# One in 42 runs of sixteen history positions fetched by SyncE, row by row, in the user stage of a recommender kernel

## The chip, the cores and the metric

The kernel runs on one core of one Trainium2 chip. The metric is the device time of one execution in microseconds; the median of three runs of the kernel before is 30,856.08 us (30,855.88 to 30,856.29). One further execution was taken with the hardware profiler, and every duration in this document that has a row of a profile beside it is from such an execution.

The engines are called as the profile calls them: PE is the TensorE, DVE the VectorE, ACT the ScalarE, POOL the GpSimd, SP the SyncE. SP does no arithmetic; in this kernel it issues plain DMAs.

## The reference, cut to what matters

There are 50,001 items and 16,384 users with 100 history positions each.

```python
# per item: two neighbour attentions over 32 neighbours
a_sus = _neighbor_attn(E_in, near_full)          # 50001 x 32
a_inf = _neighbor_attn(E_out, near_full)
# per user and history position
h = concat([E_hist[history], a_sus[history], a_inf[history]])   # 16384 x 100 x 128
t = concat([E_tgt[target],  a_inf[target],  a_sus[target]])     # 16384 x 128
z = relu(einsum('bld,hd->blh', h * t[:, None, :], W1) + b1)
exp_A = exp(einsum('blh,h->bl', z, W2[0])) * mask
attn = exp_A / (sum(exp_A, -1) ** 0.5)[:, None]
s = sum(h * attn[..., None])                     # one number
pred = dot(s, t) / (norms);  return sigmoid(pred)
```

`mask` leaves out positions whose item is the target or item 0.

## The kernel before, in words

There are two stages, one after the other.

**The item stage** works out, for all items, a row of 128 floats (64 of `E_hist`, 32 and 32 of the two attentions) and writes it to `table` in DRAM, and a second such row to `ttab` for targets. POOL gathers 30 of the 32 neighbours by indirect DMAs (L215); the other two are copied column by column from a transposed copy of the embeddings in SBUF by ACT and DVE (L229), whose addresses come from registers. The registers are loaded 32 at a time from SBUF (L189). A branch in which SP would fetch neighbours is in the code but its share is set to nought. The change leaves this stage as it is.

**The user stage** is where the change lies. The 16,384 users are laid out as 128 partitions by 128 columns; the code calls one column, which is 128 users, c, and this document calls it "user c" where the order of the work is meant. The 100 history positions of a column are cut into groups of `LW = 8`: twelve full groups and one of four, thirteen in all. The loop goes over all groups (c, g) in order, in a software pipeline of three steps:

- `gather(c, g)`: for each of the group's positions, POOL issues an indirect DMA that fetches 128 rows of 512 bytes from `table`, one for each partition (L438), into a buffer `h` of which there are six.
- `turn(c, g)`: PE transposes each position (L453), DVE multiplies by the transposed target (L455, `xT`) and sums the rows of `h` (L458, `hsum`).
- `hidden` one group later: PE multiplies by W1 (L473), ACT applies the relu (L474). `scored` two groups later: PE multiplies by W2 (L482); after the last group of a column, ACT and DVE take the exponential, the mask and two sums (L488 to L492).

Target rows of a column are one more POOL gather (L400), issued half a column ahead. The history itself, which holds the indices of the gathers, is loaded by SP for four columns at a time (L396, `hidx`, two buffers), when the target rows of a block's first column are asked for.

A column is thus 101 POOL gathers. Each engine works through its own instructions in order; a scheduling layer inserts the waits. Buffers are freed for POOL when PE and DVE have read them. The DMAs that SP issues share eight semaphores in rotation.

Of the kernel before, what the change touches and what calls it, by code (L numbers as in the profile page):

```python
# [10 lines left out]
F32 = mybir.dt.float32  # L11
I32 = mybir.dt.int32
U8 = mybir.dt.uint8
E = mybir.EngineType
AF = mybir.ActivationFunctionType
ALU = mybir.AluOpType
AX = mybir.AxisListType

P = 128
ITEMS = 50001  # L20
# [3 lines left out]
D = 128  # L24
HID = 128
B = 16384
L = 100
# [20 lines left out]
UC = B // P  # L48
BSUB = 4
LG = 4  # L50
NG = L // LG


@with_exitstack
def kernel(
# [13 lines left out]
    nc = tc.nc  # L69
# [12 lines left out]
    table = dram.tile([ROWS, D], F32, name="table")  # L82
# [30 lines left out]
    with (  # L113
# [84 lines left out]
        def gather(s):  # L198
            it, j = divmod(s, NSUB)
            nidx = its[it][0]  # L200
            v = n_v.tile([P, K, 2, G], F32, name="v")
            g = [n_g.tile([P, P], F32, name=f"g{a}") for a in range(NAUX)]
            subs[s] = {"v": v, "g": g}
            k1 = K - NAUX - 1
            by_sp = s * SPNUM % SPDEN < SPNUM
            if by_sp:
                for i0 in range(0, P, NREG):
                    vals = registers(s, 0, E.SP, i0, 0, (ITEMS - 1) * 8 * G)
                    for i in range(NREG):
                        nc.sync.dma_start(  # L210
                            v[i0 + i : i0 + i + 1, k1].rearrange("p t d -> p (t d)").bitcast(U8),
                            egeo_b[:, ds(vals[i], 8 * G)],
                        )
            for k in range(k1 if by_sp else k1 + 1):
                nc.gpsimd.indirect_dma_start(  # L215
                    out=v[:, k].rearrange("p t d -> p (t d)"),
                    out_offset=None,
                    in_=egeo,
                    in_offset=bass.IndirectOffsetOnAxis(ap=nidx[:, j, k : k + 1], axis=0),
                )  # L220
# [145 lines left out]
    hist_v = history.rearrange("(p i j) l -> i p j l", p=P, j=BSUB)  # L366
# [2 lines left out]
    tidf = const.tile([P, UC], F32, name="tidf")  # L369
    nc.vector.tensor_copy(tidf, tidx)  # L370
    with (
        tc.tile_pool(name="u_in", bufs=2) as u_in,
        tc.tile_pool(name="u_t", bufs=2) as u_t,
        tc.tile_pool(name="u_h", bufs=6) as u_h,
        tc.tile_pool(name="u_x", bufs=2) as u_x,
        tc.tile_pool(name="u_s", bufs=2) as u_s,
        tc.tile_pool(name="ps_t", bufs=2, space=bass.MemoryType.PSUM) as ps_t,
        tc.tile_pool(name="ps_z", bufs=2, space=bass.MemoryType.PSUM) as ps_z,
        tc.tile_pool(name="ps_s", bufs=2, space=bass.MemoryType.PSUM) as ps_s,
    ):  # L380
        users = {}
        hists = {}
        LW = 2 * LG
        NW = -(-L // LW)
        in_order = mybir.DependencyInfo(
            mybir.DependencyClass.NoSync, mybir.DependencyReason.DATA
        )

        def width(g):
            return min(LW, L - g * LW)  # L390

        def target_rows(c):

            if c % BSUB == 0:
                hidx = u_in.tile([P, BSUB, L], I32, name="hidx")
                nc.sync.dma_start(hidx, hist_v[c // BSUB])  # L396
                hists[c // BSUB] = hidx

            t = u_t.tile([P, D], F32, name="t")
            nc.gpsimd.indirect_dma_start(  # L400
                out=t,
                out_offset=None,
                in_=ttab[0:ITEMS, :],
                in_offset=bass.IndirectOffsetOnAxis(ap=tidx[:, c : c + 1], axis=0),
            )
            users[c] = {"t": t, "hidx": hists[c // BSUB][:, c % BSUB, :]}

        def target_work(c):
            u = users[c]
            t = u["t"]  # L410
            tT_ps = ps_t.tile([P, LG, P], F32, name="hT_ps")
            nc.tensor.transpose(tT_ps[:, 0, :], t, ident)
            tT = u_t.tile([D, 1, P], F32, name="tT")
            nc.vector.tensor_copy(tT[:, 0, :], tT_ps[:, 0, :])
            u["tT"] = tT
            nc.vector.tensor_reduce(tsum[:, c : c + 1], t, AX.X, ALU.add)
            junk = u_t.tile([P, D], F32, name="junk")
            nc.scalar.activation(junk, t, AF.Square, accum_out=tsq[:, c : c + 1])
            idf = u_s.tile([P, L], F32, name="idf")
            nc.scalar.copy(idf, u["hidx"])  # L420
            keep = u_s.tile([P, L], F32, name="keep")
            nc.vector.tensor_scalar(keep, idf, 0.0, None, ALU.not_equal)
            nc.vector.scalar_tensor_tensor(
                keep, idf, tidf[:, c : c + 1], keep, ALU.not_equal, ALU.mult
            )
            u["keep"] = keep
            u["hsum"] = u_s.tile([P, L], F32, name="hsum")
            u["score"] = ps_s.tile([P, L], F32, name="score")
            u["xT"], u["z"] = {}, {}

        def gather(c, g):
            u = users[c]
            h = u_h.tile([P, LW, D], F32, name="h")
            u["got", g] = []
            for q in range(width(g)):
                l = g * LW + q
                u["got", g].append(
                    nc.gpsimd.indirect_dma_start(  # L438
                        out=h[:, q, :],
                        out_offset=None,  # L440
                        in_=table,
                        in_offset=bass.IndirectOffsetOnAxis(ap=u["hidx"][:, l : l + 1], axis=0),
                    )
                )
            u["h", g] = h

        def turn(c, g):
            u = users[c]
            w = width(g)
            h = u.pop(("h", g))  # L450
            hT_ps = ps_t.tile([P, LW, P], F32, name="hT_ps")
            for q in range(w):
                nc.tensor.transpose(hT_ps[:, q, :], h[:, q, :], ident)  # L453
            xT = u_x.tile([D, LW, P], F32, name="xT")
            x = nc.vector.tensor_tensor(  # L455
                xT[:, 0:w, :], hT_ps[:, 0:w, :], u["tT"].to_broadcast([D, w, P]), ALU.mult
            )
            s = nc.vector.tensor_reduce(  # L458
                u["hsum"][:, g * LW : g * LW + w], h[:, 0:w, :], AX.X, ALU.add
            )  # L460

            tc.add_manual_dep(s.ins, x.ins.name, in_order, reason="after x")
            for q in u.pop(("got", g)):
                tc.declare_no_dep(s.ins, q.ins, reason="after x")
            u["xT"][g] = xT

        def hidden(c, g):
            u = users[c]
            xT = u["xT"].pop(g)
            z = u_x.tile([HID, LW, P], F32, name="z")  # L470
            for q in range(0, width(g), LG):
                z_ps = ps_z.tile([HID, LG, P], F32, name="z_ps")
                nc.tensor.matmul(z_ps, w1T, xT[:, q : q + LG, :], start=True, stop=True)  # L473
                nc.scalar.activation(z[:, q : q + LG, :], z_ps, AF.Relu, bias=b1_sb)  # L474
            u["z"][g] = z

        def scored(c, g):
            u = users[c]
            z = u["z"].pop(g)
            for q in range(width(g)):  # L480
                l = g * LW + q
                nc.tensor.matmul(  # L482
                    u["score"][:, l : l + 1], z[:, q, :], w2_sb, start=True, stop=True
                )
            if g < NW - 1:
                return
            ea = u_s.tile([P, L], F32, name="ea")
            nc.scalar.activation(ea, u["score"], AF.Exp)  # L488
            nc.vector.tensor_tensor(ea, ea, u["keep"], ALU.mult)  # L489
            nc.vector.tensor_reduce(den[:, c : c + 1], ea, AX.X, ALU.add)  # L490
            nc.vector.tensor_tensor(ea, ea, u["hsum"], ALU.mult)
            nc.vector.tensor_reduce(num[:, c : c + 1], ea, AX.X, ALU.add)  # L492
            del users[c]

        groups = [(c, g) for c in range(UC) for g in range(NW)]
        target_rows(0)
        for s in range(len(groups) + 2):
            if s < len(groups):
                c, g = groups[s]
                if g == 0:  # L500
                    target_work(c)
                if g == NW // 2 and c + 1 < UC:
                    target_rows(c + 1)
                gather(c, g)
                turn(c, g)
            if 1 <= s <= len(groups):
                hidden(*groups[s - 1])
            if s >= 2:
                scored(*groups[s - 2])
# [88 lines left out]
```

## Time and profile before

| | |
|---|---|
| median of the runs | 30,856.08 us |
| the profiled execution | 30,865.45 us |
| its span, first to last instruction | 30,863.6 us |
| user stage: first history gather starts | 14,704.9 us |
| user stage: last history gather starts | 30,845.2 us |
| POOL busy | 23,284.3 us, 75% of the span |
| PE busy (matmuls) | 13,340.6 us, 43% |
| DVE busy | 12,128.8 us, 39% |
| ACT busy | 7,843.2 us, 25% |
| TensorE clock granted in the user stage | 0.62 of full speed |

A row of a group of instructions reads: line, engine, operation, output and inputs by the program's names, count; then the busy time in us and the mean duration of one in ns; then the engine's idle time just before them and what ended most of it. "issue" is time in which the engine waited for nothing that the profile shows. A row of a line's view gives the minimum, median and maximum duration in ns, and the first and last start in us. SPq, ACTq and DVEq are the sequencers of these engines; what they do themselves (issuing a DMA, loading a register) is not counted as busy. In a timeline a row is start, duration (us), engine, line, operation, count, and in brackets the idle time before it. A row of a window has its bounds and length, and then the busy time and count of PE, of PE's weight load, of DVE, ACT and POOL, the granted clock, the busy share of the DMA engines and GB/s.

### The profile page before, as it was taken

Reading aid. Unit: us, or ns where it says so; the run is one execution under the profiler, and the core shown is the slowest. Engines: PE = TensorE matmul, PEld = TensorE weight load, DVE = VectorE, ACT = ScalarE, POOL = GpSimd, SP = SyncE. Lnnn points to the kernel's source line nnn. Section 1 sums busy time; section 2 is a strip of 40 time slices with the busy share of each in tenths; the row PEclk is TensorE's granted clock in tenths of the full one; section 3 lists DMA queues with packets and bytes.
Section 4 is the critical chain, followed back from the end, with each engine's and each line's share of the span. In section 5 each row is a group of like instructions: output and inputs, shape, how many; then the busy total and the mean of one; then the engine's idle time right before and its main releaser. Section 6 shows DMA issues by size and latency. Waiting matters only on the chain.

```text
span 30863.6 us, 246685 instructions
## 1 busy us (share of the span) xinstructions
PE 13340.6 (43%) x45932; PEld 7630.5 (25%) x45932; DVE 12128.8 (39%) x58485; ACT 7843.2 (25%) x56963; POOL 23284.3 (75%) x24664
## 2 busy tenths in 40 slices
PE   0000000000000000000778778877877877887787
PEld 0000000000000000000444444444444544454444
DVE  5555555555555555555222222222222222222222
ACT  4333333333333333333111111111111111111111
POOL 7777777777777777777777777777777777777777
PEclk9999999999999999999665666666566566656656
DMA  2111111111111111111222222222222222222221
GB/s 67 31 31 31 32 34 31 31 31 32 34 31 31 31 35 31 31 31 29 54 53 54 54 53 54 53 53 53 54 53 54 53 54 53 53 53 54 53 54 52
DMA packets 966199, 1351.82 MB, mean 44 GB/s; under 512 B 548416, under 2 KB 561280, under 8 KB 961696
## 3 DMA queue, kind: packets, MB, share of 16 engines
q0 software_dynamic: 789056, 1233.20, 17.1%
q10 hardware_dynamic: 103920, 51.31, 0.6%
q1 hardware_dynamic: 71664, 51.54, 0.6%
q14 instruction: 1192, 9.76, 0.1%
q8 instruction: 367, 6.01, 0.1%
HBM read 1295.95 MB, written 51.30 MB: 44 GB/s over the span
## 4 chain that ended last, share of the span: by engine, by line
POOL 56%; issue 23%; DMA 12%; PE 7%; DVE 1%; another core or an unknown queue 0%; ACT 0%; POOLq 0%; SPq 0%; ACTq 0%; DVEq 0%
POOL v L215 33%; POOL h L438 23%; DMA h<-table,hidx 10%; PE z_ps L473 3%; DMA v<-in_egeo_dram,nidx 2%; PE score L482 2%; PE hT_ps L453 2%; DVE xT L455 1%; DVE hsum L458 0%; DMA st<-in_egeo_dram 0%; PE pt L180 0%; POOL t L400 0%; POOLq L438 0%; ACT g L229 0%
## 5 line engine op out<-in xcount | busy, mean ns | idle before, releaser
L438 POOL DMA_INDIRECT h<-table,hidx x12800 | 12084.6, 944 | 3899.7 <-issue 3451.0
L215 POOL DMA_INDIRECT v<-in_egeo_dram,nidx x11730 | 11078.2, 944 | 3599.4 <-issue 3484.2
L453 PE MATMUL hT_ps<-ident,h 128*128 128x128 f32 x12800 | 5070.5, 414 | 3207.2 <-DMA h<-table,hidx 3025.5
L455 DVE TENSOR_TENSOR xT<-hT_ps,tT 128x1024 f32<-128x1024 f32 (+1 forms) x1664 | 1968.4, 1183 | 10942.7 <-PE hT_ps L453 10942.5
L234 PE MATMUL pt<-ident,g 128*128 128x128 f32 x782 | 363.9, 471 | 13297.0 <-DVE g L229 8118.8
L473 PE MATMUL z_ps<-xT,w1T 128*128 128x512 f32 x6400 | 5799.9, 1007 | 26.6 <-DVE xT L455 26.3
L229 ACT COPY g<-geoT 128x4 uint8 x50048 | 4919.0, 189 | 2153.7 <-issue 2152.4
L474 ACT ACTIVATE z<-z_ps,b_sb 128x512 f32<-128x512 f32 x3200 | 2201.1, 688 | 12756.3 <-PE z_ps L473 12748.7
L229 DVE COPY g<-geoT 128x4 uint8 x50048 | 3885.9, 194 | 2268.1 <-issue 2149.5
L453 PEld LDWEIGHTS hT_ps<-ident,h 128*128 128x128 f32 x12800 | 2439.0, 194 | 8517.2 <-DMA h<-table,hidx 7853.9
L482 PEld LDWEIGHTS score<-w_sb,z 128*128 128x128 f32 x25600 | 4330.9, 255 | 0.6 <-issue 0.5
L482 PE MATMUL score<-w_sb,z 128*128 128x1 f32 x25600 | 4022.1, 279 | 0.1
L234 PEld LDWEIGHTS pt<-ident,g 128*128 128x128 f32 x782 | 141.9, 183 | 13514.9 <-DVE g L229 8226.4
L258 DVE TENSOR_TENSOR prod<-v,own_ps 128x2048 f32<-128x2048 f32 x391 | 894.4, 2287 | 4148.8 <-DMA v<-in_egeo_dram,nidx 4147.6
L458 DVE TENSOR_REDUCE hsum<-h 128x8 f32<-128x1024 f32 (+1 forms) x1664 | 1942.6, 1167 | 0.0
L473 PEld LDWEIGHTS z_ps<-xT,w1T 128*128 128x128 f32 x6400 | 1884.4, 354 | 115.0 <-issue 70.4
L294 DVE TENSOR_TENSOR wv<-v,ex 128x1024 f32<-128x1024 f32 x782 | 1404.3, 1869 | 0.0
L281 ACT ACTIVATE ex<-sc,top 128x32 f32<-128x32 f32 x782 | 227.7, 291 | 4355.4 <-DVE top L273 4342.8
L268 DVE TENSOR_REDUCE sc<-prod 128x64 f32<-128x2048 f32 x391 | 894.5, 2288 | 13.5
L309 DVE TENSOR_REDUCE att<-wv 128x64 f32<-128x2048 f32 x391 | 882.9, 2258 | 0.0
L240 ACT COPY v<-pt 128x128 f32<-128x128 f32 x391 | 104.0, 266 | 2520.2 <-PE pt L234 2520.2
L489 DVE TENSOR_TENSOR ea<-ea,keep 128x100 f32<-128x100 f32 x128 | 33.8, 264 | 1177.1 <-ACT ea L488 1177.1
(67 smaller groups left out, 1536.8 us busy)
## 6 DMA issues: line engine op xcount, KB each, us to landing
h<-table,hidx POOLq DMA_INDIRECT x12800, 2.5
v<-in_egeo_dram,nidx POOLq DMA_INDIRECT x11730, 2.4
table<-row ACTq DMA_DIRECT2D x23, 1088.0 KB, 4.5
own<-in_egeo_dram SPq DMA_DIRECT2D x23, 544.0 KB, 4.0
row<-in_ehist_dram SPq DMA_DIRECT2D x23, 544.0 KB, 6.4
ttab<-trow ACTq DMA_DIRECT2D x23, 544.0 KB, 6.1
ttab<-in_etgt_dram ACTq DMA_DIRECT2D x1, 12500.0 KB, 52.4
st<-in_egeo_dram SPq DMA_DIRECT2D x65, 192.0 KB, 2.4
```

The lines of the kernel that those rows point to most:

```text
L215: nc.gpsimd.indirect_dma_start(out=v[:, k].rearrange("p t d -> p (t d)"), out_offset=None, in_=egeo, in_offset=bass.IndirectOffsetOnAxis(a ...
L229: copy(g[:, 4 * i : 4 * i + 4], geoT_b[:, ds(vals[i - i0] - geoT_at, 4)])
L258: nc.vector.tensor_tensor(prod.rearrange("p k t d -> p k (t d)"), v.rearrange("p k t d -> p k (t d)"), subs[s]["own"].to_broadcast([P, K, ...
L268: nc.vector.tensor_reduce(sc.rearrange("p t k -> p k t"), subs[s]["prod"], AX.X, ALU.add)
L294: nc.vector.tensor_tensor(subs[s]["wv"][:, t].rearrange("p d k -> p k d"), subs[s]["v"][:, :, t, :], subs[s]["ex"][0][:, t, :] .rearrange( ...
L438: nc.gpsimd.indirect_dma_start(out=h[:, q, :], out_offset=None, in_=table, in_offset=bass.IndirectOffsetOnAxis(ap=u["hidx"][:, l : l + 1], ...
L453: nc.tensor.transpose(hT_ps[:, q, :], h[:, q, :], ident)
L455: x = nc.vector.tensor_tensor(xT[:, 0:w, :], hT_ps[:, 0:w, :], u["tT"].to_broadcast([D, w, P]), ALU.mult)
L458: s = nc.vector.tensor_reduce(u["hsum"][:, g * LW : g * LW + w], h[:, 0:w, :], AX.X, ALU.add)
L473: nc.tensor.matmul(z_ps, w1T, xT[:, q : q + LG, :], start=True, stop=True)
L474: nc.scalar.activation(z[:, q : q + LG, :], z_ps, AF.Relu, bias=b1_sb)
L482: nc.tensor.matmul(u["score"][:, l : l + 1], z[:, q, :], w2_sb, start=True, stop=True)
```

## The change

SP fetches some of the rows that POOL gathered. The twelve full groups of a column are taken in pairs (`UG = 2`), so there are 6 pairs a column and 768 in all; every 42nd of them (`UNIT`), 18 in all, is a unit that SP fetches. For a unit, DVE works out the byte offsets of 16 positions in all 128 partitions (the item's number shifted left by 9, `hoff`). Then, for each partition, SP loads its sixteen offsets into registers and issues sixteen DMAs of one row of 512 bytes each, into a buffer `hs` of which there are two: 128 register loads and 2,048 DMAs for a unit. The unit's two groups are then taken from `hs`, and POOL issues no gathers for them.

The fetch of a unit is written down one unit ahead: that of unit k+1 at the place of unit k in the loop, that of the first ahead of the loop. The history must be there earlier for this, so its loads move out of `target_rows`: four blocks are loaded ahead of the loop, and each later one four blocks (16 columns) ahead of its use, with six buffers where there were two. They stay on SP and are kept in the order of the program.

```diff
+UG = 2
+UNIT = 42
+AHEAD = 4
-        tc.tile_pool(name="u_in", bufs=2) as u_in,
+        tc.tile_pool(name="u_in", bufs=AHEAD + 2) as u_in,
+        tc.tile_pool(name="u_hs", bufs=2) as u_hs,
...
+        table_b = table.bitcast(U8).rearrange("(o r) d -> o (r d)", o=1)
+
+        def history_of(i):
+            hidx = u_in.tile([P, BSUB, L], I32, name="hidx")
+            tc.keep_in_program_order(nc.sync.dma_start(hidx, hist_v[i]))
+            hists[i] = hidx
+
         def target_rows(c):
-            if c % BSUB == 0:
-                hidx = u_in.tile([P, BSUB, L], I32, name="hidx")
-                nc.sync.dma_start(hidx, hist_v[c // BSUB])
-                hists[c // BSUB] = hidx
...
+        def one_by_one(c, g):
+            hs = u_hs.tile([P, UG * LW, D], F32, name="hs")
+            hoff = u_hs.tile([P, UG * LW], I32, name="hoff")
+            nc.vector.tensor_scalar(
+                hoff, hists[c // BSUB][:, c % BSUB, g * LW : (g + UG) * LW],
+                9, None, ALU.logical_shift_left,
+            )
+            for p in range(P):
+                _, vals = nc.values_load_multi_w_load_instructions(
+                    hoff[p : p + 1, :], engines=[E.SP],
+                    min_val=0, max_val=(ITEMS - 1) * 4 * D,
...
+                )
+                for q in range(UG * LW):
+                    nc.sync.dma_start(
+                        hs[p : p + 1, q, :].bitcast(U8), table_b[:, ds(vals[q], 4 * D)]
+                    )
+            for i in range(UG):
+                early[c, g + i] = hs[:, i * LW : (i + 1) * LW, :]
+
         def gather(c, g):
             u = users[c]
+            if (c, g) in early:
+                u["h", g] = early.pop((c, g))
+                u["got", g] = []
+                return
...
         groups = [(c, g) for c in range(UC) for g in range(NW)]
+        units = [(c, g) for c in range(UC) for g in range(0, NW - UG + 1, UG)]
+        units = units[UNIT - 1 :: UNIT]
+        for i in range(AHEAD):
+            history_of(i)
+        one_by_one(*units[0])
         target_rows(0)
         for s in range(len(groups) + 2):
+            if s % (BSUB * NW) == 0 and AHEAD + s // (BSUB * NW) < UC // BSUB:
+                history_of(AHEAD + s // (BSUB * NW))
+            if s < len(groups) and groups[s] in units[:-1]:
+                one_by_one(*units[units.index(groups[s]) + 1])
             if s < len(groups):
                 c, g = groups[s]
```

More of the change, by code (lines that the diff above doesn't have):

```diff
@@ L429, in target_work @@
             u["xT"], u["z"] = {}, {}
+        early = {}
+        def one_by_one(c, g):
+            hs = u_hs.tile([P, UG * LW, D], F32, name="hs")
+            hoff = u_hs.tile([P, UG * LW], I32, name="hoff")
+            nc.vector.tensor_scalar(
+                hoff,
+                hists[c // BSUB][:, c % BSUB, g * LW : (g + UG) * LW],
+                9,
+                None,
+                ALU.logical_shift_left,
+            )
+            for p in range(P):
+                _, vals = nc.values_load_multi_w_load_instructions(
+                    hoff[p : p + 1, :],
+                    engines=[E.SP],
+                    min_val=0,
+                    max_val=(ITEMS - 1) * 4 * D,
+                    skip_runtime_bounds_check_because="worked out from an item's number",
+                )
[5 more added lines that the diff above has]
+                early[c, g + i] = hs[:, i * LW : (i + 1) * LW, :]
         def gather(c, g):
             u = users[c]
+            if (c, g) in early:
+                u["h", g] = early.pop((c, g))
+                u["got", g] = []
+                return
             h = u_h.tile([P, LW, D], F32, name="h")
```

## The prediction

> **What bounds the kernel now.** I read the page's slices and its chain first. POOL is at 7 tenths in all forty slices, and the chain that ended last goes through POOL and its issue time; in the user stage TensorE is busy but waits for rows.
>
> ```profile
> POOL 7777777777777777777777777777777777777777
> POOL 56%; issue 23%; DMA 12%; PE 7%; DVE 1%; another core or an unknown queue 0%; ACT 0%; POOLq 0%; SPq 0%; ACTq 0%; DVEq 0%
> L438 POOL DMA_INDIRECT h<-table,hidx x12800 | 12084.6, 944 | 3899.7 <-issue 3451.0
> L453 PE MATMUL hT_ps<-ident,h 128*128 128x128 f32 x12800 | 5070.5, 414 | 3207.2 <-DMA h<-table,hidx 3025.5
> ```
>
> The reader is to see that a history gather is 944 ns busy and that the time ahead of it is "issue", not a wait. The order of POOL's instructions near the end of the stage gives the period.
>
> ```profile
> 30844.00 0.94 POOL L438 DMA_INDIRECT h<-table,hidx  x1 [0.30 <-issue]
> 30845.25 0.95 POOL L438 DMA_INDIRECT h<-table,hidx  x1 [0.30 <-issue]
> ```
>
> L438's first and last gather start at 14,704.9 and 30,845.2 us, with 12,800 history and 128 target gathers between: 16,140.3 / 12,927 = 1.2486 us each, without a break. So the user stage is a count of POOL gathers times 1.2486 us, plus 18.4 us of tail. A window of 998 us in its middle shows the rest below its limit:
>
> ```profile
> 20000.00:20998.00 998.00, 774.16 (x2778) 436.91 (x2778) 244.87 (x270) 142.77 (x230) 754.55 (x800) 0.65 0.20 53
> ```
>
> That is 100 groups of eight positions (9.98 us each): TensorE 7.7 us per group, VectorE 2.4, ScalarE 1.4, the DMA engines 20%. The DMA queue's own waits show SP idle:
>
> ```profile
> SPq L396 <- DMA h<-table,hidx: 15120.0, 90, 504.6
> ```
>
> **What the change takes from POOL.** The 768 pairs of full groups (six per user) are counted off, each 42nd is fetched by SP: pairs 41, 83, ... 755, that is 18 units and 18 x 16 = 288 gathers: 288 x 1.2486 = 359.6 us. If SP always delivers in time, this is the whole effect: 30,863.6 - 359.6 = 30,504 in the profiled span. TensorE must then work two groups for which POOL spends no time: it falls 2 x 7.7 = 15.5 us behind, catches up 2.2 us per group, and POOL, at 10 us a group, needs under two of its six h buffers meanwhile. That is hidden; without this slack it would cost up to 15.5 us a unit.
>
> **What it adds to SP, and where that lies.** Per unit 2,048 DMAs of one 512-byte row and 128 loads of sixteen registers; the built program has nothing else between them but one or two history loads and one wait for the hs buffer per unit. Call the time of one unit T. SP starts unit k+1 when VectorE has made its offsets, at the place of unit k in the order of groups. From there to unit k+1 there are 7 users less 16 gathers: 7 x 101 - 16 = 691 POOL gathers = 862.8 us. So T below about 863 us is hidden behind POOL; above it TensorE waits for hs, POOL fills its six h buffers and stops too, and SP sets the pace. SP then never pauses (offsets and buffer for the next unit are ready while it is on this one), and the end is 14,705 (stage start, when the table is written and SP can begin) + 18 T + what follows the last unit. That is user 125's last four positions and users 126 and 127: 204 positions, some 44 of them already gathered in the six buffers, so about 161 gathers = 201 us, plus some 20 us to work through the unit, plus the tail of 18.4: 240 us. Span = 14,945 + 18 T. It meets the old 30,863.6 at T = 884.4; each microsecond of T beyond costs 18.
>
> **T, term by term.** The trace of before has no DMA with an address from a register and no single-row DMA. The nearest rows are SP's own plain DMAs.
>
> ```profile
> 14701.48 0.81 SPq L396 DMA_DIRECT2D hidx<-in_history_dram  x2
> L396 SPq DMA_DIRECT2D hidx<-in_history_dram x32: 327/328/425, 14701.5 to 29840.2; - x32
> L189 ACTq TENSOR_LOAD <-cols x1564: 1948/1978/5590, 171.7 to 14631.3; - x196
> L189 DVEq TENSOR_LOAD <-cols x1564: 2097/2144/2361, 55.8 to 14655.3; - x196
> ```
>
> A history load holds SP 327 to 425 ns. The two side by side take 0.81 us; the second is the 425, so the first and the gap are 0.385 us from start to start, a gap of about 0.05. Bounds for a row: 0.327 (no gap; a smaller transfer than 128 rows might be cheaper still, which no row shows) and 0.475 (each one like the second of the pair, 0.425 + 0.05). I take 0.385, the spacing of the nearest row, with nothing for the register: 2,048 x 0.385 = 788.5 us.
>
> A load of 32 registers takes 1.978 us on ScalarE's queue and 2.144 on VectorE's; SP has none. Sixteen cost between half of the shorter, 0.99, and all of it, 1.98. If registers come one after another, half is the nearer; with a 0.05 gap 1.04 us: 128 x 1.04 = 133.1 us. [...]
>
> T = 788.5 + 133.1 = 921.6 us. 18 T = 16,589; span 31,534; that is +670 against 30,863.6. The profiled execution's own time is 30,865.45 and the median of the runs 30,856.08; the difference carries over: 30,856 + 670 = **31,526 us** (+2.2%).
>
> [...]
>
> **Edits with one answer.** The offset shift, 18 VectorE instructions of about 198 ns (the row of the shift `coli<-nidx`), 3.6 us in all under VectorE's 75% idle. The history loads: 32 SP DMAs as before, now queued behind up to a unit of rows (0.9 ms), four blocks of four users ahead: 16 x 101 x 1.2486 = 2,018 us, so still in time; they wait for gathers that are long past. If this cover went, ScalarE's idf and POOL's gathers of a block would wait for the rest of a unit. At 0.4 us each they add at most 0.8 to T. TensorE's longer lists of waits ahead of an early pair: some ten waits of tens of ns, 18 times. The first unit: its rows start with the stage and its place comes after about 687 gathers, 858 us, as the others'.
>
> **In flight.** The built program gives SP's DMAs eight semaphores in rotation and each row waits for the one eight before it. History loads land 2.4 us after issue: 2.4 / 8 = 0.30 us a row, below the 0.385 that issuing takes. It would bind from 3.08 us on; gathers land in 2.4 to 3.9. The DMA engines' 20% leaves room; POOL's period holds whatever the landing is.
>
> **Rivals.**
> - *SP delivers in time; POOL stays the bound.* T below 864: a row at 0.355 with the 1.04 load would do. For it: it moves one row where a history load moves 128 longer ones; SP is idle for 15.1 ms of the stage; an undisturbed DMA holds SP only 0.327 (T = 803 without gaps). Against: the plain DMAs of 1,536, 1,600 and 2,176 bytes a row all hold SP 327 to 337 ns, so size hardly counts and the 0.05 gap was there each time. Time 30,856 - 360 = 30,496. This is the case on the other side; it decides below T = 884.
> [...]
> - *A wash.* T between 881 and 888, within 0.2%: POOL's saving is given back as waiting. 30,856.
>
> **How the numbers follow.** 0.2% (62 us) is about what a measurement here can tell from no change. SP sets the pace with T of 888 to 1,000, the forecast: 0.38. In time, or nearly: 0.37. Much slower: 0.21. Wash: 0.04. Faster 0.37, same 0.04, slower 0.59. The predicted time is that of the likeliest case, 31,526, whose own range is 30,920 (T = 888) to 32,940 (T = 1,000). The two signs hold nearly even chances, so the range for 8 in 10 reaches from 30,480 (a few us under the full saving) to 33,600, a T of 1,037: the rule's price, and 30 us above it for a dearer register load; the held-up pair at 34,845 is left out with part of the last case.
>
> **What would show it.** 288 fewer POOL gathers, still at 1.2486 us while POOL runs. SP's row DMAs: duration and start-to-start give 0.385 right or wrong; 2,304 register loads give 1.04. If SP sets the pace, units come 922 us apart, PE shows waits at L453 for DMA hs of about 60 us each, POOL waits for PE and VectorE at a full set of h buffers, and SP has no wait longer than a row's. If POOL stays the bound, SP waits once per unit for the VectorE offsets, for 863 - T, and units stand 863 us apart. The prediction is wrong if a row DMA from a register takes 0.355 us or less (faster), or 0.43 and more (well above).

## The result: 0.45% faster, where 2.2% slower was forecast

| | before | after |
|---|---|---|
| median of the runs, us | 30,856.08 | 30,719.06 (30,715.38 to 30,719.56) |
| ratio, 95% interval | | 0.9955 (0.9941 to 0.997) |
| span of the profiled execution, us | 30,863.6 | 30,713.5 |
| POOL gathers in the user stage | 12,928 | 12,640 |
| their first start, us | 14,702.4 | 14,694.9 |
| their last start, us | 30,845.2 | 30,694.7 |

The forecast was 31,526 us. The time lies within the stated range, which took in both signs, and on the other side of no change. It is near neither of the two large cases: the saving counted for POOL was 359.6 us, and the medians lie 137.0 apart. The profiled spans lie 150.1 apart, because the profiled execution of before was 9.4 us above its median and that of after 3.7 below.

### The profile after

These are rows of the page of the changed kernel: POOL's busy tenths and groups of instructions.

```profile
POOL 7777777777777777777777777777777777777777
L479 POOL DMA_INDIRECT h<-table,hidx x12512 | 11806.8, 944 | 3827.7 <-issue 3235.9
L494 PE MATMUL hT_ps<-ident,h 128*128 128x128 f32 x12512 | 4558.6, 398 | 2837.7 <-DMA h<-table,hidx 2665.9
L514 PE MATMUL z_ps<-xT,w1T 128*128 128x512 f32 x6400 | 5598.4, 982 | 893.9 <-DVE xT L496 893.7
L424 DVE TENSOR_REDUCE tsum<-t 128x1 f32<-128x128 f32 x128 | 35.6, 278 | 970.2 <-DMA t<-ttab,tidx 958.3
```

A history gather still takes 944 ns. The 288 gathers are gone: 12,512 + 128 are left. POOL was idle 3,899.7 us ahead of 12,800 history gathers and is idle 3,827.7 us ahead of 12,512: by count it should be 87.7 us less, and it is 72 less. What the saving lost lies elsewhere, and two other rows that were not among the costly ones point to it: TensorE waits 893.7 us for VectorE's `xT`, and VectorE waits 958.3 us for target rows at a reduction that is 278 ns long. The page's chain, which carried the reading of before, breaks off at its end here (0% on every engine), so the next views stand in its place.

The line's view of SP's own instructions gives the terms of the prediction's T (minimum, median and maximum ns, first and last start in us):

```profile
L454 SPq TENSOR_LOAD <-hoff x2304: 1140/1257/1531, 14699.8 to 30013.5; - x192
L462 SPq MOVE hs<-table x36864: 29/29/38, 14701.0 to 30019.7; - x200
L462 SPq DMA_DIRECT2D hs<-table x36864: 224/228/332, 14701.1 to 30019.8; - x200
```

A row is two instructions: a register move of 29 ns and a DMA of 228. Between the rows of one partition it is 0.323 us from start to start in the median and 0.332 in the mean; from the last row ahead of a register load to the first behind it 1.663 in the mean. So 15 x 0.332 + 1.663 = 6.64 us for one partition, and x 128 = 850 us for a unit. The starts of the 18 units lie 851.2 us apart, below the 862.8 us of POOL's gathers between two units. SP is therefore in time, and gains on the others: the first unit is used 17 us after its last row was issued, the last one 418 us after. PE's matmuls wait for no row of `hs`; its weight loads do 26 times, 0.6 us at most.

The waits of three engines, as line waited for, total us, times, longest us:

```profile
DVE tsum L424 <- DMA t<-ttab,tidx: 958.3, 18, 53.5
PE z_ps L514 <- DVE xT L496: 893.7, 84, 49.4
POOL t L408 <- ACT z L515: 214.4, 25, 13.3
```

VectorE has eighteen of these waits, as many as there are units, and POOL loses 11 to 13 us behind each. The timeline around the first unit shows one of them:

```profile
15562.26 1.40 PE L494 MATMUL hT_ps<-ident,hs 128*128 128x128 f32 x11
...
15607.80 0.94 POOL L479 DMA_INDIRECT h<-table,hidx  x1 [0.31 <-issue]
15609.05 0.94 POOL L408 DMA_INDIRECT t<-ttab,tidx  x1 [0.30 <-issue]
15611.54 0.29 DVE L424 TENSOR_REDUCE tsum<-t 128x1 f32<-128x128 f32 x1 [53.42 <-DMA t<-ttab,tidx]
15611.74 1.22 DVE L496 TENSOR_TENSOR xT<-hT_ps,tT 128x1024 f32<-128x1024 f32 x1
15613.01 2.07 PE L514 MATMUL z_ps<-xT,w1T 128*128 128x512 f32 x2 [49.35 <-DVE xT L496]
15622.16 0.27 PE L420 MATMUL hT_ps<-ident,t 128*128 128x128 f32 x1
15623.18 0.94 POOL L408 DMA_INDIRECT t<-ttab,tidx  x1 [13.19 <-ACT z L515]
15624.43 0.94 POOL L479 DMA_INDIRECT h<-table,hidx  x1 [0.30 <-issue]
```

The unit is the last pair of column c, here 6, and PE transposed the first 11 of its 16 positions at 15,562. On VectorE the first thing behind that is not the unit's product (L496) but the sum of the target rows of column c+2 (L424), which POOL asks for only at 15,609. VectorE stands still for 53.42 us, PE with it. POOL goes on, but only as far as its buffers: the four positions that end column c and five groups of column c+1 are 44 gathers, 55 us, and fill all six `h` buffers. Then come two target gathers side by side, those of c+2 and c+3. The second needs one of the two `t` buffers, that of column c+1, whose last reader is PE's transpose of these targets (15,622.16), behind the whole stall; the row names ACT's L515, which doesn't read `t`. POOL pauses, and from the first to the second of the pair it is 14.1 us where 1.25 would do.

The last unit, in column 125, has no target gather of a column c+3 behind it. There POOL stops at a history gather, with the six `h` buffers alone:

```profile
30483.70 0.94 POOL L408 DMA_INDIRECT t<-ttab,tidx  x1 [0.30 <-issue]
30496.23 0.94 POOL L479 DMA_INDIRECT h<-table,hidx  x1 [11.59 <-PE hT_ps L494]
```

The trace has exactly 18 such gaps, 12.5 to 14.2 us from start to start, 240.5 us in all. That closes the account: 18 ordinary periods would be 22.5, so 218.0 us are lost, and 359.6 - 218.0 = 141.6 are gained. From its first gather to its last the stage is 143.1 us shorter. All other gathers stand 1.2487 us apart (before 1.2488): SP's 36,864 DMAs don't slow them.

The order is made by the scheduling layer. In the program the gather of a column's targets stands half a column ahead of its use, and in the built kernel before it still does. There the largest wait of a target gather for a buffer is 0.3 us:

```profile
POOL t L400 <- ACT z L474: 4.3, 14, 0.3
```

In the built kernel after, the sum stands ahead of the unit at all 18 units, and the two gathers stand together at the 17 that have a column c+3.

The same window as before, of 998 us, holds one such gap:

```profile
20000.00:20998.00 998.00, 757.16 (x2908) 449.30 (x2907) 256.78 (x285) 149.08 (x240) 744.51 (x790) 0.66 0.19 54
```

POOL made 790 gathers where there were 800, for it lost its 12 us. TensorE did more than before (2,908 matmuls against 2,778): the window holds a unit, on which POOL spent nothing, and it opens 13 us after the end of a stall, with part of that backlog still to be done.

### The profile page after: what moved, and what is told of

It is laid out like the page before. It is cut to its first block, busy times and chain, and to the rows that moved or that the text cites. A ratio compares the mean times of both kernels' runs of the same rounds, so it can differ in the third digit from the quotient of the medians.

```text
span 30713.5 us, 322553 instructions
## 1 busy us (share of the span) xinstructions
PE 12699.1 (41%) x45932; PEld 7403.5 (24%) x45932; DVE 12136.2 (40%) x58503; ACT 7842.4 (26%) x56963; POOL 22999.3 (75%) x24376
## 5 line engine op out<-in xcount | busy, mean ns | idle before, releaser
L479 POOL DMA_INDIRECT h<-table,hidx x12512 | 11806.8, 944 | 3827.7 <-issue 3235.9
L514 PE MATMUL z_ps<-xT,w1T 128*128 128x512 f32 x6400 | 5598.4, 982 | 893.9 <-DVE xT L496 893.7
L496 DVE TENSOR_TENSOR xT<-hT_ps,tT 128x1024 f32<-128x1024 f32 (+1 forms) x1664 | 1969.1, 1183 | 10040.1 <-PE hT_ps L494 10040.1
L494 PE MATMUL hT_ps<-ident,h 128*128 128x128 f32 x12512 | 4558.6, 398 | 2837.7 <-DMA h<-table,hidx 2665.9
L515 ACT ACTIVATE z<-z_ps,b_sb 128x512 f32<-128x512 f32 x3200 | 2198.5, 687 | 11907.6 <-PE z_ps L514 11903.6
L523 PEld LDWEIGHTS score<-w_sb,z 128*128 128x128 f32 x25600 | 4132.8, 244 | 179.7 <-issue 166.8
L494 PEld LDWEIGHTS hT_ps<-ident,h 128*128 128x128 f32 x12512 | 2260.8, 188 | 7361.2 <-DMA h<-table,hidx 6777.0
L523 PE MATMUL score<-w_sb,z 128*128 128x1 f32 x25600 | 3833.2, 273 | 0.0
L514 PEld LDWEIGHTS z_ps<-xT,w1T 128*128 128x128 f32 x6400 | 1809.1, 336 | 1149.5 <-DVE xT L496 918.8
L424 DVE TENSOR_REDUCE tsum<-t 128x1 f32<-128x128 f32 x128 | 35.6, 278 | 970.2 <-DMA t<-ttab,tidx 958.3
```

Of the source, the lines that this page charges most:

```text
L479: nc.gpsimd.indirect_dma_start(out=h[:, q, :], out_offset=None, in_=table, in_offset=bass.IndirectOffsetOnAxis(ap=u["hidx"][:, l : l + 1], ...
L496: x = nc.vector.tensor_tensor(xT[:, 0:w, :], hT_ps[:, 0:w, :], u["tT"].to_broadcast([D, w, P]), ALU.mult)
L523: nc.tensor.matmul(u["score"][:, l : l + 1], z[:, q, :], w2_sb, start=True, stop=True)
```

## The experiments

**Theory A:** POOL is the bound as before and SP is in time; the order of the target gathers and sums, which the scheduling layer made, takes 218 us of the 360. **Rival B:** SP's stream of DMAs costs the others time, on queues, buffers or the DMA engines, and the order is only where it shows. **Rival C:** SP is late at some units after all. In five batches the kernel before itself took 40,260 to 40,620 us. These are called held up here: in such a batch 599 gathers of the kernel before (with both pins of below) stand over 3 us from the one ahead, and in the trace of before none does. So each kernel is compared with the kernel before of its own batch, and only the batches at some 30,860 us say what A and B cost in the runs of the result.

### The target gather held in its place

```diff
-            nc.gpsimd.indirect_dma_start(
+            tc.keep_in_program_order(nc.gpsimd.indirect_dma_start(
                 out=t, out_offset=None, in_=ttab[0:ITEMS, :], ...
-            )
+            ))
```

> The changed kernel with POOL's target gather (L408) kept in its place, once more. Where the kernel before takes 30,860 us, theory A (order): about 30,500 (30,480 to 30,530); theories B (row DMAs slow the gathers) and C (SP is late): 30,719. Where the sequencers pause (the kernel before at 40,300 to 40,600): 44,900 to 45,500, SP the bound, and the question stays as the planted order left it.

Measured: 30,503.18 us (30,502.46 to 30,503.7) against 30,858.16; ratio 0.9885 (0.9869 to 0.9902). From the views of its waits:

```profile
DVE tsum L426 <- DMA t<-ttab,tidx: 502.7, 18, 28.1
PE z_ps L516 <- DVE xT L498: 39.9, 64, 1.0
POOL t L409 <- issue: 57.9, 114, 23.4
POOL t L409 <- ACT z L517: 4.3, 14, 0.3
```

And from its timeline and page, the target gather after the first unit, and the gathers as a group:

```profile
15623.79 0.94 POOL L409 DMA_INDIRECT t<-ttab,tidx  x1 [0.30 <-issue]
15626.41 0.29 DVE L426 TENSOR_REDUCE tsum<-t 128x1 f32<-128x128 f32 x1 [28.09 <-DMA t<-ttab,tidx]
...
L481 POOL DMA_INDIRECT h<-table,hidx x12512 | 11807.0, 944 | 3817.5 <-issue 3485.4
```

POOL's wait for a target buffer is 0.3 us at most (the 23.4 us of issue stand ahead of the stage's first gather), and among 12,640 gathers no two neighbours stand more than 3 us apart. VectorE still waits 18 times for target rows, 28 us each, but no longer ahead of a unit's product; POOL's buffers cover 28 us, as they didn't cover 53, and the wait costs nothing. SP's stream is the same as in the changed kernel (rows 0.332 us apart in the mean, units 851.3), the units are used 862.8 us apart, the number that the prediction counted from the gathers, and the gain is 355.0 of the 359.6. Theory A holds: the pin is worth 355.0 - 137.0 = 218 us, each gain counted against the kernel before of its own batch, and 218.0 is what the 18 gaps had cost. For B nothing is left in the user stage: from first gather to last it takes 15,783.1 us where it took 16,142.9, which is 359.8 less. Where the 4.6 us lie that the medians lack wasn't found. This version is faster than both kernels.

### The order planted where SP does next to nothing

To see whether the order costs time without SP's rows, a unit is fetched here by one plain DMA of 2,048 consecutive rows (not the rows that the history names; no offsets, no loads), and there are 64 units so that an effect is large. The first kernel holds the gathers in their places; the second is the same with the order of the changed kernel planted by hand.

```diff
-UNIT = 42
+UNIT = 12
...
-            for p in range(P):
-                _, vals = nc.values_load_multi_w_load_instructions(...)
-                for q in range(UG * LW):
-                    nc.sync.dma_start(hs[p : p + 1, q, :]..., table_b[:, ds(vals[q], 4 * D)])
+            nc.sync.dma_start(hs, table[0 : P * UG * LW, :].rearrange("(p q) d -> p q d", p=P))
```

and in the second kernel

```diff
...
+                tc.add_manual_dep(first.pop(c - 2).ins, total.ins.name, in_order, ...)
...
-                if g == NW // 2 and c + 1 < UC:
+                if c > 0 and c % 2 == 0 and g == 5:
                     target_rows(c + 1)
...
+                if c > 0 and c % 2 == 0 and g == 5 and c + 2 < UC:
+                    target_rows(c + 2)
```

> A stand-in without SP's stream: one unit in 12 pairs (64 units, the last pair of every second column), each fetched by one plain DMA of 2,048 consecutive table rows, so the output is not the reference's; the target gathers (L409) are kept in the program's place. It is the base for the next run: 1,024 gathers fewer at about 1.58 us, some 1,600 us below the kernel before (about 39,000 where that takes 40,590), less what TensorE can't follow (as much as half of it).

> The same with the order of the changed kernel planted at every unit: the sum of the rows of the target after next stands ahead of the unit's products on DVE, and the gather after that one stands beside it on POOL (two history gathers between). Nothing else differs, and SP issues no more than one DMA a unit. Theory A (this order is what gave the gain back): POOL waits 8 to 14 us at the second target gather in nearly every unit, DVE 50 to 80 us at the sum; 64 units cost at least 500 us, more where TensorE can't catch up: 500 to 3,000 us above planted_none. Against A (the order only moves waiting about): within 150 us of planted_none.

Measured in one batch, against 30,861.47: 29,589.07 us, ratio 0.9588 (0.9572 to 0.9604), and with the order planted 30,195.68, ratio 0.9785 (0.9768 to 0.9801). The first has 1,024 gathers fewer, 1,278.6 us, and gains 1,272.4: TensorE can follow, where the expectation allowed for a loss of up to half. The second gives 606.6 back, 9.6 us for each of 63 stalls, within theory A's 500 to 3,000 and far from the 150 of the case against it. The first kernel's waits, and then the second's:

```profile
POOL h L464 <- PE z_ps L499: 170.1, 558, 0.3
PE z_ps L499 <- DVE xT L481: 17.7, 34, 0.9
```

```profile
DVE tsum L426 <- DMA t<-ttab,tidx: 3366.5, 63, 53.6
PE z_ps L506 <- DVE xT L486: 3093.1, 64, 50.7
POOL h L469 <- PE z_ps L506: 697.2, 360, 9.9
```

Nothing of SP's rows is left, and VectorE's wait is there in the same size, 53.6 us. The loss is smaller than the 12.1 us of the changed kernel, and its place is another:

```profile
15467.27 0.94 POOL L409 DMA_INDIRECT t<-ttab,tidx  x1 [0.30 <-issue]
15478.01 0.94 POOL L469 DMA_INDIRECT h<-table,hidx  x1 [9.80 <-PE z_ps L506]
```

Here two history gathers ended up between the two target gathers, and POOL stops at the first of them, for an `h` buffer. The changed kernel's further 2 us are not the `t` buffer: at its last unit POOL also stops for an `h` buffer, and the gap is 12.5 us against 10.7 here. The traces differ in the unit itself. Here its two products on VectorE start 2.3 us apart (15,470.05 and 15,472.31), and at the changed kernel's first unit 6.6 us apart (15,611.74 and 15,618.32), the second one waiting for PE's transposes. That this makes the difference fits the traces and wasn't tried by itself.

Why the layer orders it so wasn't shown. With one plain DMA for a unit, and the gathers held, VectorE has no such wait at all; that the layer reckons 2,048 small DMAs to be later than they are, and so puts other work ahead of their readers, is only an argument.

### The same and other edits, in the held-up batches

In these runs SP sets the pace, or rows of SP cost more than the order does, so they can't tell A from B. The pin of the target gather is the edit above; the others:

```diff
 # sums held in place
+            tc.keep_in_program_order(nc.vector.tensor_reduce(tsum[:, c : c + 1], t, ...))
+            tc.keep_in_program_order(nc.scalar.activation(junk, t, AF.Square, ...))
 # units in the middle of a column
-        units = units[UNIT - 1 :: UNIT]
+        units = units[UNIT - 4 :: UNIT]
```

> The changed kernel with one edit: POOL's gather of a column's target rows (L408) is kept where the program writes it, behind all that POOL was given before. In the changed kernel the scheduling layer puts, around each unit, two of these gathers side by side, and the sum of the later one's rows (L424) on DVE ahead of the unit's products. Theory A (order): DVE waits some 50 us for those rows and POOL then waits 13 us for a buffer, 18 times; without it 18 x 12 = 220 us come back: about 30,500 us (30,490 to 30,530). Theory B (the row DMAs slow the gathers or the landing): nothing changes, 30,719. Theory C (SP is late): nothing changes either, 30,719, and PE waits for hs.

> The changed kernel with another edit: not the gather but its readers are kept in the program's place, DVE's sum (L424) and ACT's sum of squares (L426). Theory A: DVE can no longer stand before a unit waiting for rows of a later column; the same gain by the other end, about 30,500 us (30,490 to 30,540). Theories B and C: 30,719.

> The changed kernel with the units moved from the last pair of a column (groups 10 and 11) to its third (groups 4 and 5); as many units, as many rows, the same spacing. The scheduling layer now puts two sums ahead of the unit on DVE, and the later gather stands six groups on in POOL's order, just where the six h buffers are used up. Theory A: DVE waits about 60 us per unit, POOL stops at the full buffers for another 18 to 24 us: 18 x 20 = 360 us lost of the 360 saved, about 30,860 us (30,780 to 30,930). Theories B and C do not depend on the place: 30,719.

> The kernel before with both pins (the target gather, and its readers on DVE and ACT). Theory A: in the kernel before the gathers stand where the program has them, and nothing waits there; the pins are worth nothing by themselves: 30,856 (30,840 to 30,875). If they gained here too, the gain of the two runs above would not be the change's.

| edit | us | before, us | ratio, 95% |
|---|---|---|---|
| gather pinned | 44,950.01 | 40,343.64 | 1.1149 (1.1133 to 1.1164) |
| sums pinned | 44,988.7 | 40,343.64 | 1.1152 (1.1137 to 1.1167) |
| units in the middle | 45,094.92 | 40,343.64 | 1.1182 (1.1165 to 1.1199) |
| both pins in the kernel before | 40,399.38 | 40,343.64 | 1.001 (1.0001 to 1.002) |

All four were expected near 30,500 to 30,860 us; the first three came out 14,200 to 14,500 us higher, the fourth some 9,500. The fourth says that the pins gain nothing in the kernel before: with them it is 0.1% slower. Three of the edits were run again in later batches, with these expectations:

> The pin of POOL's target gather (L408) once more: in the first batch every engine's sequencer was slow on that chip (the kernel before took 40,344 us there against 30,856), SP's unit took 1,366 us and set the pace, so the theories could not be told apart. At the kernel before's usual 30,856 us: theory A (order) 30,500 us (30,490 to 30,530); theories B (row DMAs slow the gathers) and C (SP is late) 30,719.

> The units in the middle of the column once more, for the same reason. Theory A: DVE waits about 60 us before each unit for the rows of a later column, POOL stops at six full buffers for 18 to 24 us more: about 30,860 us (30,780 to 30,930). Theories B and C do not depend on the place: 30,719.

> POOL's target gather (L408) kept in its place, a third time, in search of a chip on which the kernel before takes its usual 30,856 us. There: theory A (order) 30,500 us (30,490 to 30,530); theories B (row DMAs slow the gathers) and C (SP is late) 30,719. If the kernel before takes about 40,350 us again, the result is near 44,950, SP's unit about 1,366 us and SP the bound, as in the two batches ahead.

> The changed kernel with POOL's target gather (L408) kept in its place, where the kernel before takes 30,860 us. Theory A (order): the 18 waits of 13.4 us at the second target gather go, less the 1.25 us that each gather takes anyway: 18 x 12.1 = 218 us: 30,719 - 218 = about 30,500 (30,480 to 30,530). Theory B (row DMAs slow the gathers) and theory C (SP is late): 30,719. Where the sequencers pause: about 44,950, SP the bound.

> The changed kernel with the readers of the target rows (DVE's sum, ACT's sum of squares) kept in the program's place and the gather left free. Theory A: the scheduling layer then leaves the gathers one by one as well; about 30,500 (30,480 to 30,540). Theories B and C: 30,719. Where the sequencers pause: about 44,990.

> The units in the middle of the column (groups 4 and 5). The later target gather stands six groups on in POOL's order, after as many gathers as there are h buffers. Theory A: DVE waits about 60 us, POOL stops at the full buffers for 18 to 24 us a unit: 18 x 20 = 360 us lost of the 360 saved: about 30,860 (30,780 to 30,930). Theories B and C do not depend on the place: 30,719. Where the sequencers pause: about 45,090.

They were held up too: gather pinned 44,996.13, 44,917.2 and 45,456.9 us, ratios 1.1149, 1.1154 and 1.1189; units in the middle 45,089.0 and 45,532.67, 1.1171 and 1.1209; sums pinned 45,462.65, 1.1192. Whether the sums' pin and the other place of the units work as the gather's does in undisturbed runs stays open.

The changed kernel itself was then run in such a batch, with half as many units (with and without the pin), and with rows at fixed addresses, without register loads, in which both pins are kept and the rows aren't those of the history:

```diff
 # half as many units
-UNIT = 42
+UNIT = 84
 # rows at fixed addresses
-                _, vals = nc.values_load_multi_w_load_instructions(...)
...
-                        hs[p : p + 1, q, :].bitcast(U8), table_b[:, ds(vals[q], 4 * D)]
+                        hs[p : p + 1, q, :].bitcast(U8), table_b[:, ds((p * UG * LW + q) * 4 * D, 4 * D)]
```

> The changed kernel itself, unedited, on the chips of the experiments, where the kernel before takes about 40,350 us and every engine's sequencer pauses between instructions. Its unit of rows should take about 1,366 us there as in the pinned kernel, against a spacing of 691 gathers at the 1.572 us that a gather takes on these chips, 1,086 us: SP sets the pace, and the order of the target gathers does not matter behind it. Theory A (order) and theory C (SP late) both: 44,950 (44,850 to 45,100). If the pins were what made the kernel slow there, it would come out near 40,200.

> The changed kernel with one unit in 84 pairs, 9 in all, in the order that the scheduling layer gives (the sum of a later column's target rows still stands ahead of each unit on DVE, two target gathers side by side on POOL). The spacing is then over 2,100 us and SP, at about 1,366 us a unit, is in time. 144 gathers at 1.572 us are saved: 226 us. Theory A: 9 times 12 to 25 us come back as POOL's wait at the second target gather: about 40,250 to 40,330 where the kernel before takes 40,350. Theory B (row DMAs slow the gathers): no gap at the target gathers, but a longer gather. Without either: 40,125.

> The same with POOL's target gather (L408) kept where the program writes it. Theory A: no wait at the target gathers; 100 to 220 us less than every_84th, about 40,125 (40,050 to 40,200) where the kernel before takes 40,350. Theory B: as every_84th.

> The pinned kernel (one unit in 42) with the row DMAs kept but their addresses fixed when the program is built: no register loads, and rows that are not those of the history, so the output is not the reference's. Asked: what the register costs a row. In the profile of the changed kernel a row is a 0.029 us register move and a 0.228 us DMA, 0.322 us from start to start. If the DMA's part stays 0.228 and the move goes, the start-to-start is about 0.26 us where nothing pauses; if a fixed address is dearer or as dear as the 0.385 us that I took from the history loads, it is 0.33 to 0.39. The load's share, 128 times 1.3 us a unit, goes in either case.

> The pinned kernel with row DMAs from fixed addresses and no register loads; the rows are not those of the history, so the output is not the reference's. Row from start to start: 0.29 us if the paused chips' median holds (0.295 there, against 0.323 from a register), so a unit of 2,048 x 0.295 = 604 us against 851. POOL stays the bound as in the pinned kernel: about 30,500. The difference of the units, 247 us, is then 128 loads at about 1.48 and 2,048 moves at 0.028.

| kernel | us | ratio to 40,593.18 |
|---|---|---|
| changed kernel, unedited | 45,459.57 | 1.1195 (1.1177 to 1.1214) |
| half as many units | 41,208.58 | 1.0151 (1.0134 to 1.0168) |
| the same, gather pinned | 41,188.82 | 1.0143 (1.0126 to 1.016) |
| fixed addresses, no loads (one run) | 41,047.49 | 1.0112 |

The unedited kernel's SP lines and waits in this batch:

```profile
L462 SPq MOVE hs<-table x36864: 1/29/1422, 20202.0 to 45226.0; - x200
L462 SPq DMA_DIRECT2D hs<-table x36864: 1/228/1422, 20202.0 to 45226.0; - x200
```

```profile
PE hT_ps L494 <- DMA hs<-table: 4209.4, 19, 251.6
POOL t L408 <- ACT z L515: 4138.5, 17, 259.5
```

The medians are those of the other runs, 29 and 228 ns; single instructions take up to 1.42 us, and the mean distance of two rows is 0.609 us where it was 0.332. A unit takes 1,390.7 us. POOL's 691 gathers between two units would take 691 x 1.572 = 1,086, an estimate with the period in the trace of the kernel before with both pins, from another batch. PE begins on each unit some 3.6 us before SP issues its last row, as soon as the first position has landed in all partitions: PE waits for SP, 4,209 us in all, and POOL's waits stand behind PE's. This is rival C, and the very mechanism of the forecast, where T does exceed POOL's spacing. The forecast's formula with these numbers (stage start 20,202, 18 x 1,391, some 290 behind the last unit) gives 45,530; the span was 45,516. The time is 360 us above the upper end of what was expected, for the unit takes 1,391 us and not 1,366.

With half as many units SP has time (a unit is complete some 690 us ahead of its use), and the two kernels differ in POOL's wait for a target buffer. The first line is in the kernel without the pin, the second in that with it:

```profile
POOL t L408 <- ACT z L515: 98.3, 8, 13.0
```

```profile
POOL t L409 <- issue: 149.1, 128, 110.4
```

The eight waits are gone (the 110.4 us stand ahead of the stage's first gather), and the total is 20 us less, within the intervals, where theory A had 100 to 220. The pair decides nothing, for 98 us are 0.24% here. Both kernels came out some 900 to 1,000 us above the ranges that were expected, of which the slower batch explains some 240. They are slower than the kernel before though they have 144 gathers fewer. So is the kernel with fixed addresses (in its second batch 41,077.08 us, 1.0111), where PE waits for `hs` 29 us in all and SP loads no register. Its rows answer what the register costs:

```profile
L461 SPq DMA_DIRECT2D hs<-table x36864: 2/250/1427, 20202.0 to 39477.3; - x200
```

From row to row it is 0.295 us in the median, against 0.324 from a register in the same batch. So an address from a register costs a row 0.029 us there, as much as the move. The 0.26 that was expected is missed, because the DMA itself is 250 ns there and not 228.

In these batches rival B is real. With the 1.572 us of above for a gather, 40,593 less 144 x 1.572 is 40,367, and 41,209 is 842 more, for 38,016 instructions of SP; with fixed addresses it is 907 more for 36,864. By this estimate it comes to 0.022 and 0.025 us for each instruction that SP issues. In the undisturbed run 4.6 us are missing with 76,032.

## Why the prediction was wrong

**The count for POOL: right.** 288 gathers were worth 359.6 us; with the order mended 355.0 arrived. In the undisturbed runs gathers keep their period under SP's rows, the catching up of TensorE at a unit is hidden, and the history loads behind SP's rows delay nothing. One reading is off by a trifle: two of the 128 target gathers lie ahead of the first history gather, so the period is 16,140.3 / 12,925 = 1.2488 us, which changes the saving by less than 0.1.

**"T, term by term": the step that failed.** T was 788.5 + 133.1 = 921.6 and is 2,048 x 0.332 + 128 x 1.331 = 680 + 170 = 850. Two terms were off in opposite directions:
- The row was taken at 0.385, from a pair of plain DMAs whose first was 0.327 long. It is 0.332, 109 us less for a unit. The register's address is not free, as was assumed, but a move of 29 ns; the DMA behind it is 0.228, shorter than any row of the trace of before. The prediction named "a smaller transfer ... might be cheaper still, which no row shows" and then set its lower bound at a plain DMA's 0.327; the measured spacing lies just above that bound in the mean and below it in the median (0.323), the DMA well below it.
- The load was taken at half of a load of 32 and is 1.257 us; with the gaps it adds 1.331, 37 us more for a unit.

The forecast turned on the side of 884 us on which T lies, and 850 is on the other; it is also below the 863 of POOL's gathers, so SP was in time. By the prediction's own mark, 0.355 for a row, the rival "SP delivers in time" was the case; it was given 0.37. The upper end of the stated range, a T of 1,037, and with it the "much slower" that was given 0.21, holds a price of a row that no run shows, and 30 us a unit for a dearer load; in the undisturbed run a row is 0.228 for the DMA and 0.332 with everything around it, the load is 37 us a unit dearer, and T is 850.

**The term that no case had: a step that failed too.** The rival "SP delivers in time" said 30,496. It is 7 us from the kernel with the gather pinned and 223 from the changed kernel. The prediction read the built order of SP, and of the other engines only the count of what went; "edits with one answer" costed each in the place that the source gives it. The built order of VectorE and POOL had moved: the sum ahead of the unit and the two target gathers side by side. The prediction put this at nothing; it is 12.1 us at each of 18 units, 218 us. The check that "POOL needs under two of its six `h` buffers" was right for a catch-up of 15.5 us and not asked for a stall of 53.

**The signs that were named.** Units 863 us apart if POOL stays the bound: 862.8 with the pin, 875.0 without, and the difference is the loss of 12 us at a unit. "SP waits once per unit for the VectorE offsets, for 863 - T": after the first it had no such wait. In the built kernel the offsets of a unit are made when the unit two before it is used (the second unit's at 14,700.5, the third's at 15,622.7), as early as the two buffers allow, and not one unit ahead as in the source; so SP could gain on the rest unit by unit.

## What to carry to other kernels

Where a change hands work to another engine under a scheduling layer, read the built order of every engine around the new work, not only of the engine that gets it: a reader of late data that is put ahead of a reader of early data costs nothing until the buffers behind it are full, and then at every turn (here nothing for a wait of 28 us, and 12.1 us at each of 18 turns for one of 53). When a forecast hangs on one engine's rate against another's spacing and the two lie as near as 922 and 863 us do here, the rows of the nearest operation don't decide the sign; measure the new form's cost first. One pinned instruction can be worth more than the change itself: 218 us against 137 here.

## What the runs showed of the hardware that wasn't expected

- A DMA of one 512-byte row with its address in a register holds SP 228 ns, after a 29 ns move; a plain history load of 128 rows held it 327 to 425 in the trace of before. Rows come every 0.323 us in the median. With a fixed address it is 250 ns and 0.295 in a held-up batch, where a row from a register comes every 0.324.
- A load of sixteen registers on SP takes 1.257 us in the median (1.140 to 1.531), more than half of the 1.978 for 32 on ScalarE's queue.
- 36,864 such DMAs, three or four to each gather of POOL, left the gathers' period at 1.2487 us in the undisturbed run.
- In the held-up batches the kernel before takes 30 to 32% longer, and SP's stream costs, by the estimate above, 0.022 to 0.025 us of the whole for each of its instructions, though it shares no data with the others until a unit is done. What holds the engines up was not found.
